# Selective scan in half groups: kept decays, one load a step, and a new order of GpSimd, TensorE and ScalarE work

## The chip, the cores and the metric

The kernel is one program on one core of a Trainium2 chip. The metric is the time on the device in microseconds (us), from the first to the last instruction of the run; less is better. The core has five engines that run side by side, each through its own instructions in order: TensorE (PE in the profile, its weight loads PEld), VectorE (DVE), ScalarE (ACT), GpSimd (POOL) and SyncE (SP), which here does nothing but issue DMA transfers. They meet only through semaphores: an instruction waits until another engine, or a DMA, has counted one up.

## The reference

Four images of 64 x 64 pixels and 96 channels go through four layers. The first is a Mamba-like layer, whose core is a selective scan over the L = 4096 pixels of an image, for 192 inner channels with 16 states each:

```python
def step(h, inp):
    u_t, dt_t, B_t, C_t = inp
    dA = jnp.exp(dt_t[..., None] * A)
    h = dA * h + (dt_t * u_t)[..., None] * B_t[:, None, :]
    y = jnp.sum(h * C_t[:, None, :], axis=-1)
    return (h, y)
```

It runs four times for an image: over the rows and over the columns, each forward and backward. The four results are added up, gated and projected. The layers after it are a 3 x 3 depthwise convolution with a pointwise one, linear attention with a feed-forward part in emulated fp8, and a frequency filter (Fourier transform, gate, inverse) with a second such feed-forward part.

## The kernel before, in words

**Half groups.** The scan takes 8 inner channels x 16 states = 128 partitions at a time. One `n` of the main loop (`for n in range(N + 1)`, N = 192) is one image, one order of the pixels (rows or columns) and one group of 8 channels, forward and backward. 24 values of `n` in a row share an image and an order; such a run of 24 is a half. The 4096 pixels are cut into four chunks `q` of 1024.

**Eight steps to an n.** Steps q0 to q3 are the forward scans of chunks 0 to 3 (VectorE, L1677, into S). Steps k0 to k3 are the backward scans of chunks 3, 2, 1, 0 (L1722, written over the decays), each followed by an addition of the backward states to S (L1729). The helpers around them are:

- `load_delta`, `load_du` (both issue at L1412): replicated loads. One chunk of 8 channels is spread over 128 partitions by two DMAs of 256 KB. `load_rep` (L1435) does it for B and C of a half, which stay for 24 values of n.
- `decay` (L1450): ScalarE, exp(dt * A) of a chunk from `dl` into a PSUM tile `pa` of two banks; there are two such tiles.
- `times_b` (L1440): GpSimd multiplies dt * u by B, in the tile `B`. `times_c` (L1444): GpSimd multiplies the summed states S by C.
- `reduce` (L1460): TensorE sums over the 16 states into the PSUM tile `py` (one bank, one buffer); `result` (L1468): ScalarE copies it out; `store_result` (L1477) sends it to memory.

PSUM is full: 4 banks for the two `pa` tiles, 1 for `py`, 3 for everything else. A forward scan of chunk 3 leaves its decays in PSUM for the backward scan; those of chunks 2, 1 and 0 are computed a second time. So there are seven `decay` calls to an n.

**The order is written out by hand.** Inside `tc.manual_schedule()` each engine runs the instructions as the loop emits them. The tiles of one tag reuse one buffer, so a load waits for the last reader of the chunk before it. `place_of` and the tag of `B` alternate with n, so that a chunk's place is free when the next half group's chunk needs it.

**Side work.** Everything else of the four images (projections and the 3 x 3 convolution ahead of the scans of an image, gating and all later layers after them) is cut into pieces, which two lanes hand out between the steps. `pieces(step)` gives each of five resources (TensorE, ScalarE, GpSimd, VectorE, the SP queue) a credit, in estimated us, from the table `gains`, one row for each of the eight steps; a piece is emitted when its resources have credit. ScalarE's copies of the pieces wait for TensorE's matmuls of the pieces, and stand in ScalarE's queue ahead of the next `decay`. Until about n = 54 the pieces are the projections and convolutions of images 1 to 3; later they are the layers after the scan of images 0 to 2. What is left of them after the last scan, and all later layers of image 3, run then: first `drain` with `last_post` (L619 to L625), then `tail`, which begins with the convolution L833.

Of the kernel before, what the change touches and what calls it, by code (L numbers as in the profile page):

```python
# [73 lines left out]
def layers(ctx: ExitStack, tc: tile.TileContext, a: dict, out):  # L74
# [1268 lines left out]
    def main_lane(take):  # L1343

        region = Region(tc)
        wk = region.sbuf("pre")
        images = [before_scans(b, wk, take, prev=b - 1 if b > 1 else None) for b in range(1, NB)]
        yield [chain(*parts) for parts in zip(*images)], [region, weights]
        for b in range(NB - 1):
            yield from rest(b, take, 1)  # L1350
# [17 lines left out]
    def last_place(name, k):  # L1368

        if (name, k) not in last_tiles:  # L1370
            tags = {
                "w_in": [f"B{4 * (N % 2) + q}" for q in range(4)],
                "sz_in": [f"dl{place_of(N - 1, q)}" for q in (3, 2, 1, 0)],
# [72 lines left out]
    def decay(n, q):  # L1446
        if n < N:
            pa = ps.tile([128, CH], F32, tag="pa", name="pa", bufs=2)
            g = phases[n][1]
            nc.scalar.activation(pa, dls[n, q], AF.Exp, scale=nega[:, g : g + 1])  # L1450
            return pa

    def reduce(n, half):
# [3 lines left out]
        py = pys[n, half] = ps.tile([128, BLK], F32, tag="py", name="py")  # L1457
        for j in range(4):
            q, k = 2 * half + j // 2, j % 2
            nc.tensor.matmul(  # L1460
                py[32 * j : 32 * j + 32, :], lhsT=red, rhs=Ss[n, q][:, k * BLK : (k + 1) * BLK],
                start=True, stop=True,
            )
# [19 lines left out]
    class Lane:  # L1483
# [133 lines left out]
    def first_loads():  # L1617
# [10 lines left out]
        for q in range(3):  # L1628
# [17 lines left out]
    with tc.manual_schedule():  # L1646
        ordered[0] = True
        pa = decay(0, 0)
        for n in range(N + 1):
# [3 lines left out]
            for q in range(NCH):  # L1653

                if q == 1:
                    load_du(n + 1, 3)
                if q > 1:
                    load_delta(n + 1, q - 2)
                if n % NG == 0 and 0 < n < N and q > 0:
                    load_rep(h, 1, 4 - q)  # L1660
                later = decay(n, q + 1) if q < 3 else decay(n, 2)
                if q == 0:
                    times_c(n - 1, 0)
                elif q == 1:
                    times_b(n, 3)
                else:
                    times_b(n + 1, q - 2)
                if q == 1:
                    reduce(n - 1, 0)
                if q == 2:  # L1670
                    store_result(n - 1, 1)
                if end:
# [5 lines left out]
                    s, pa, Bs[n, q], Ss[n, q - 1][:, CH - 1 : CH] if q else 0.0, ALU.mult, ALU.add  # L1678
                )
                if q < 3:  # L1680
                    pa = later
# [18 lines left out]
            for k, q in enumerate(reversed(range(NCH))):  # L1700
                if k == 0:
                    times_b(n + 1, 2)
                    result(n - 1, 0)
                    load_delta(n + 1, 2)
                else:
                    times_c(n, q + 1)
                if k == 1:
                    store_result(n - 1, 0)
                if k == 2:
                    load_delta(n + 1, 3)  # L1710
                if k > 0:
                    load_du(n + 2, k - 1)
                if n % NG == NG - 2:
                    load_rep(h + 1, 0, k)
                if k == 1:
                    pa, later = later, decay(n, 1)
                elif k == 2:
                    pa, later = later, decay(n, 0)
                elif k == 3:
                    pa, later = later, decay(n + 1, 0)  # L1720

                nc.vector.tensor_tensor_scan(  # L1722
                    pa[:, ::-1], pa[:, ::-1], Bs[n, q][:, ::-1],
                    edge if k else 0.0, ALU.mult, ALU.add,
                )
                if k < 3:
                    edge = big.tile([128, 1], F32, tag="edge", name="edge", bufs=2)
                    nc.vector.tensor_copy(edge, pa[:, 0:1])
                nc.vector.tensor_tensor(Ss[n, q], Ss[n, q], pa, ALU.add)  # L1729
# [6 lines left out]
            pa = later  # L1736
# [121 lines left out]
```

## Time and profile before

| | |
|---|---|
| time, median of 3 runs (lowest to highest) | 5908.66 us (5899.17 to 5910.47) |
| the profiled execution's own time | 5897.32 us |
| its span, first to last instruction | 5895.5 us |
| first and last scan begin at | 359.2 us, 5483.8 us |
| VectorE busy | 4947.4 us, 84% |
| GpSimd busy | 4104.8 us, 70% |
| TensorE busy | 4072.8 us, 69% |
| ScalarE busy | 3235.1 us, 55% |
| DMA queue of SP | 1169 MB, 71.7% of 16 engines |

A group of the profile is told by its line and engine, with output and inputs by name, the shape, the count, the busy time, the mean duration of one, and the idle time of the engine just before them with its main releaser. A row of waits says who waited for whom, for how long in total, how many times, and the longest. Some VectorE groups cost 1.2 to 2.4 us apiece, so a wait of a few tenths is small beside a step, and 192 of them are not small beside the total.

### The profile page before, as it was taken

The numbers are of one execution on the slowest core, as the hardware profiler recorded it, in microseconds if no ns is written. First come the engines' busy times: TensorE is split into PE (matmuls) and PEld (weight loads), VectorE is DVE, ScalarE is ACT, GpSimd is POOL, SyncE is SP. The second block draws the span as 40 slices with busy tenths as digits, with TensorE's granted clock in tenths as the row PEclk, the third lists the DMA queues.
The fourth block names the chain that finished last, engine by engine and source line by source line (L and its number), as shares of the span: only waits on it lengthen the run. The fifth ranks groups of instructions, "written<-read, shape, count | busy, mean of one in ns | idle before, by whom it ended". The sixth has DMA issues, their size and how long they took to land. (4 is left out here: it accounts for less than half of the span.)

```text
span 5895.5 us, 64395 instructions
## 1 busy us (share of the span) xinstructions
PE 4072.8 (69%) x19490; PEld 1646.2 (28%) x19490; DVE 4947.4 (84%) x3590; ACT 3235.1 (55%) x4358; POOL 4104.8 (70%) x1982
## 2 busy tenths in 40 slices
PE   8978888889873675553566764656467655566787
PEld 3322222223220121142321211433122114332245
DVE  2049898899899998999899999999998999989464
ACT  4557766776664356545555456454634554545333
POOL 1258888889898667767678778776866777766300
PEclk9978888889875765566657865676576655785788
DMA  3258878887698878788988868686986568896203
GB/s 99 77 158 236 226 208 223 244 243 206 187 248 238 229 199 222 202 227 246 254 228 229 211 169 222 203 239 187 239 224 182 158 190 234 248 242 184 57 30 112
DMA packets 469416, 1173.08 MB, mean 199 GB/s; under 512 B 90496, under 2 KB 155628, under 8 KB 468972
## 3 DMA queue, kind: packets, MB, share of 16 engines
q1 hardware_dynamic: 469068, 1168.97, 71.7%
q8 instruction: 154, 2.52, 0.2%
q14 instruction: 194, 1.59, 0.1%
HBM read 1011.86 MB, written 156.76 MB: 198 GB/s over the span
## 5 line engine op out<-in xcount | busy, mean ns | idle before, releaser
L1444 POOL TENSOR_TENSOR S<-S,rep 128x1024 f32<-128x1024 f32 x768 | 1807.1, 2353 | 965.1 <-DVE S L1729 885.1
L1450 ACT ACTIVATE pa<-dl,nega 128x1024 f32<-128x1024 f32 x1344 | 1498.5, 1116 | 1539.1 <-DVE S L1729 1175.0
L1440 POOL TENSOR_TENSOR B<-B,rep 128x1024 f32<-128x1024 f32 x768 | 1790.8, 2359 | 90.5 <-DMA B<-du_s 45.3
L1677 DVE TENSOR_TENSOR_SCAN S<-pa,S,B 128x1024 f32<-128x1024 f32 x576 | 1352.1, 2347 | 257.3 <-ACT pa L1450 86.1
L1722 DVE TENSOR_TENSOR_SCAN pa<-pa,edge,B 128x1024 f32<-128x1024 f32 x576 | 1354.0, 2351 | 66.7 <-ACT pa L1450 66.6
L1460 PE MATMUL py<-S,red 128*32 128x512 f32 x3072 | 630.9, 886 | 858.9 <-POOL S L1444 785.1
L361 PE MATMUL p_conv<-xp,conv_w 96*96 96x504 f32 (+3 forms) x2304 | 1056.4, 613 | 13.6 <-ACT u L374 11.5
L1729 DVE TENSOR_TENSOR S<-S,pa 128x1024 f32<-128x1024 f32 x768 | 932.2, 1214 | 6.6
L1677 DVE TENSOR_TENSOR_SCAN S<-pa,B 128x1024 f32<-128x1024 f32 x192 | 438.0, 2281 | 176.7 <-DMA rep<-bc_s 173.1
L361 PEld LDWEIGHTS p_conv<-xp,conv_w 96*96 96x96 f32 x2304 | 386.1, 171 | 669.0 <-issue 615.5
L1722 DVE TENSOR_TENSOR_SCAN pa<-pa,B 128x1024 f32<-128x1024 f32 x192 | 440.8, 2296 | 5.3
L1460 PEld LDWEIGHTS py<-S,red 128*32 128x32 f32 x3072 | 76.0, 128 | 1228.0 <-POOL S L1444 1009.6
L154 ACT COPY side<-side 96x256 f32<-96x256 f32 (+1 forms) x448 | 281.3, 628 | 52.9 <-DMA duT_s<-side 25.9
L1055 POOL CAST h<-y 128x1536 fp8e5<-128x1536 f16 x64 | 95.5, 1493 | 294.7 <-ACT y L766 284.2
L877 PE MATMUL p_mean<-t,centre 96*96 96x512 f32 x256 | 199.5, 895 | 117.7 <-ACT sq L869 48.8
L527 PE MATMUL p_y<-side,ident 96*96 96x512 f32 x336 | 215.2, 792 | 29.9 <-DMA side<-y_s 15.6
L1468 ACT COPY ys<-py 128x512 f32<-128x512 f32 x384 | 221.2, 576 | 19.6 <-PE py L1460 17.3
L929 PE MATMUL p_rstd<-rs_y,pick 32*96 32x512 f32 x256 | 168.4, 985 | 71.0 <-DVE ln L920 23.6
L833 PE MATMUL p_l<-x,taps 96*96 96x504 f32 (+3 forms) x432 | 202.8, 623 | 9.6 <-DMA x<-x 9.6
L1120 PE MATMUL p_h<-w1s,ln 97*64 97x64 f32 x2304 | 177.9, 346 | 36.7 <-DVE hb L1104 18.6
L1046 PE MATMUL p_f<-q,w_L 96*128 96x512 fp8e5 x192 | 98.2, 548 | 149.7 <-ACT y L757 75.6
L1120 PEld LDWEIGHTS p_h<-w1s,ln 97*64 97x64 f32 x2304 | 171.6, 251 | 78.2 <-issue 31.4
(210 smaller groups left out, 5059.4 us busy)
## 6 DMA issues: line engine op xcount, KB each, us to landing
dl<-delta_s SPq DMA_DIRECT2D x768, 256.0 KB
B<-du_s SPq DMA_DIRECT2D x768, 256.0 KB
B<-duT_s SPq DMA_DIRECT2D x768, 256.0 KB
dl<-deltaT_s SPq DMA_DIRECT2D x768, 256.0 KB
z_s<-z SPq DMA_DIRECT2D x48, 512.0 KB
zl<-z_s SPq DMA_DIRECT2D x64, 384.0 KB
side<-y_s SPq DMA_DIRECT2D x120, 192.0 KB
rep<-bc_s SPq DMA_DIRECT2D x64, 256.0 KB
```

The costliest lines, as they stand in the source:

```text
L154: nc.scalar.copy(o.rearrange("p (w h) -> p w h", h=HW), t[:n, :].rearrange("p (h w) -> p w h", w=HW)[:, q * w : (q + 1) * w, :],)
L361: nc.tensor.matmul(pr[:, ra:rb, ca_:cb_], lhsT=conv_w[:, kc, ky * 3 + kx, oc * C : (oc + 1) * C], rhs=xp[:, kc, at + ra : at + rb, ca_ + d ...
L527: nc.tensor.matmul(p, lhsT=ident[:C, :C], rhs=x, start=(j == 0), stop=(j == 2))
L1120: nc.tensor.matmul(p[at : at + N1, j, :], lhsT=ln3[:, 8 * k + j, :], rhs=w1s[:, hs], start=True, stop=True,)
L1440: nc.gpsimd.tensor_tensor(Bs[n, q], Bs[n, q], reps[n // NG, 0, q], ALU.mult)
L1444: nc.gpsimd.tensor_tensor(Ss[n, q], Ss[n, q], reps[n // NG, 1, q], ALU.mult)
L1450: nc.scalar.activation(pa, dls[n, q], AF.Exp, scale=nega[:, g : g + 1])
L1460: nc.tensor.matmul(py[32 * j : 32 * j + 32, :], lhsT=red, rhs=Ss[n, q][:, k * BLK : (k + 1) * BLK], start=True, stop=True,)
L1468: nc.scalar.copy(ys, pys.pop((n, half)))
L1677: nc.vector.tensor_tensor_scan(s, pa, Bs[n, q], Ss[n, q - 1][:, CH - 1 : CH] if q else 0.0, ALU.mult, ALU.add)
L1722: nc.vector.tensor_tensor_scan(pa[:, ::-1], pa[:, ::-1], Bs[n, q][:, ::-1], edge if k else 0.0, ALU.mult, ALU.add,)
L1729: nc.vector.tensor_tensor(Ss[n, q], Ss[n, q], pa, ALU.add)
```

## The change

- **Decays.** `decay` gets two tags of one buffer each, paX and paY, in place of one tag with two buffers, and a flag that tells which. The decays of chunk 2 are no longer computed a second time: those of chunks 2 and 3 both stay in PSUM from the forward scan to the backward one. Six calls remain to an n.
- **GpSimd.** Before, q0 to k3: C of the n before on chunk 0; B of chunk 3; B of the next n on chunk 0; on chunk 1; on chunk 2; C of chunk 3; of chunk 2; of chunk 1. After: q0 B of chunk 3; q1 C of the n before on chunk 0; q2 nothing; q3 B of the next n on chunk 0; k0 on chunk 1; k1 on chunk 2, and C of chunk 3; k2 C of chunk 2; k3 C of chunk 1.
- **TensorE.** The sum over chunks 0 and 1 of the n before, which stood in q1 as a whole, is split: chunk 1 in q1, chunk 0 in q3. ScalarE copies it out in k0, as before.
- **Loads.** Before: q1 du 3, q2 delta 0, q3 delta 1, k0 delta 2, k1 du 0, k2 delta 3 and du 1, k3 du 2 (the du of k1 to k3 are for the n after the next one, the others for the next). After: q0 du 2, q1 du 3, q2 delta 2, q3 delta 1, k0 delta 0, k1 du 0, k2 delta 3, k3 du 1.
- **Side work.** The table `gains` is new: TensorE's credit for an n stays 23.2 us, GpSimd's and VectorE's stay, ScalarE's rises from 14.3 to 15.5 us, SP's falls from 9.8 to 9.4 us. `sz_in` of the last image takes other tiles.

```diff
@@ -1370,7 +1371,7 @@
         if (name, k) not in last_tiles:
             tags = {
                 "w_in": [f"B{4 * (N % 2) + q}" for q in range(4)],
-                "sz_in": [f"dl{place_of(N - 1, q)}" for q in (3, 2, 1, 0)],
+                "sz_in": [f"dl{place_of(*x)}" for x in ((N - 1, 3), (N - 1, 2), (N - 1, 1), (N, 0))],
                 "xr": [f"rep0{q}" for q in range(4)],
                 "y_in": [f"B{4 - 4 * (N % 2) + q}" for q in range(4)],
             }
@@ -1443,19 +1444,23 @@
         if n >= 0:
             nc.gpsimd.tensor_tensor(Ss[n, q], Ss[n, q], reps[n // NG, 1, q], ALU.mult)
 
-    def decay(n, q):
+    def decay(n, q, first):
+
         if n < N:
-            pa = ps.tile([128, CH], F32, tag="pa", name="pa", bufs=2)
+            tag = "pa" + "XY"[(n + (not first)) % 2]
+            pa = ps.tile([128, CH], F32, tag=tag, name="pa")
             g = phases[n][1]
             nc.scalar.activation(pa, dls[n, q], AF.Exp, scale=nega[:, g : g + 1])
             return pa
 
-    def reduce(n, half):
+    def reduce(n, half, chunks=(0, 1)):
 
         if n < 0:
             return
-        py = pys[n, half] = ps.tile([128, BLK], F32, tag="py", name="py")
-        for j in range(4):
+        if (n, half) not in pys:
+            pys[n, half] = ps.tile([128, BLK], F32, tag="py", name="py")
+        py = pys[n, half]
+        for j in (2 * c + k for c in chunks for k in range(2)):
             q, k = 2 * half + j // 2, j % 2
             nc.tensor.matmul(
                 py[32 * j : 32 * j + 32, :], lhsT=red, rhs=Ss[n, q][:, k * BLK : (k + 1) * BLK],
@@ -1516,10 +1521,10 @@
     credit = [0.0] * 5
 
     gains = [
-        (2.6, 0.7, 0, 0.8, 1.8), (1.4, 1.2, 0, 0.8, 0.8),
-        (2.6, 1.2, 0, 0.8, 0.8), (2.6, 1.2, 0, 0.8, 0.8),
-        (3.8, 2.8, 1.2, 1, 1.6), (3.8, 2.4, 1.2, 1, 1.4),
-        (3.8, 2.4, 1.2, 1, 1.0), (2.6, 2.4, 1.2, 1, 1.6),
+        (2.6, 0.7, 0, 0.8, 1.4), (2.0, 1.2, 0, 0.8, 0.8),
+        (2.6, 1.2, 0, 0.8, 0.8), (2.0, 2.0, 0, 0.8, 0.8),
+        (3.8, 3.0, 1.2, 1, 1.4), (3.8, 2.6, 1.2, 1, 1.4),
+        (3.8, 2.4, 1.2, 1, 1.4), (2.6, 2.4, 1.2, 1, 1.4),
     ]
     cap = (4.4, 3.0, 3.2, 1.6, 4.0)
 
@@ -1625,7 +1630,7 @@
                 times_b(0, q)
         for q in range(NCH):
             load_rep(0, 1, q)
-        for q in range(3):
+        for q in range(2):
             load_du(1, q)
 
     wk = head.sbuf("pre0")
@@ -1645,40 +1650,40 @@
 
     with tc.manual_schedule():
         ordered[0] = True
-        pa = decay(0, 0)
+        pas = [decay(0, 0, True), None, None, None]
         for n in range(N + 1):
             h = n // NG
             end = n == N
 
             for q in range(NCH):
 
-                if q == 1:
-                    load_du(n + 1, 3)
-                if q > 1:
-                    load_delta(n + 1, q - 2)
+                if q < 2:
+                    load_du(n + 1, q + 2)
+                else:
+                    load_delta(n + 1, 4 - q)
                 if n % NG == 0 and 0 < n < N and q > 0:
                     load_rep(h, 1, 4 - q)
-                later = decay(n, q + 1) if q < 3 else decay(n, 2)
+                if q < 3:
+                    pas[q + 1] = decay(n, q + 1, q == 1)
                 if q == 0:
+                    times_b(n, 3)
+                elif q == 1:
                     times_c(n - 1, 0)
-                elif q == 1:
-                    times_b(n, 3)
+                    reduce(n - 1, 0, (1,))
+                elif q == 2:
+                    store_result(n - 1, 1)
                 else:
-                    times_b(n + 1, q - 2)
-                if q == 1:
-                    reduce(n - 1, 0)
-                if q == 2:
-                    store_result(n - 1, 1)
+                    times_b(n + 1, 0)
+                    reduce(n - 1, 0, (0,))
                 if end:
                     if q == 0:
                         result(n - 1, 1)
                     continue
                 s = Ss[n, q] = big.tile([128, CH], F32, tag=f"S{place_of(n, q)}", name="S")
                 nc.vector.tensor_tensor_scan(
-                    s, pa, Bs[n, q], Ss[n, q - 1][:, CH - 1 : CH] if q else 0.0, ALU.mult, ALU.add
+                    s, pas[q], Bs[n, q], Ss[n, q - 1][:, CH - 1 : CH] if q else 0.0,
+                    ALU.mult, ALU.add,
                 )
-                if q < 3:
-                    pa = later
                 pieces(q)
                 if q == 0:
                     result(n - 1, 1)
@@ -1698,42 +1703,45 @@
                 done["half", NB - 1] = True
 
             for k, q in enumerate(reversed(range(NCH))):
+                if k < 2:
+                    times_b(n + 1, k + 1)
+                if k > 0:
+                    times_c(n, q + 1)
                 if k == 0:
-                    times_b(n + 1, 2)
                     result(n - 1, 0)
-                    load_delta(n + 1, 2)
+                    load_delta(n + 1, 0)
+                elif k == 1:
+                    store_result(n - 1, 0)
+                    load_du(n + 2, 0)
+                elif k == 2:
+                    load_delta(n + 1, 3)
                 else:
-                    times_c(n, q + 1)
-                if k == 1:
-                    store_result(n - 1, 0)
-                if k == 2:
-                    load_delta(n + 1, 3)
-                if k > 0:
-                    load_du(n + 2, k - 1)
+                    load_du(n + 2, 1)
                 if n % NG == NG - 2:
                     load_rep(h + 1, 0, k)
                 if k == 1:
-                    pa, later = later, decay(n, 1)
+                    pas[1] = decay(n, 1, False)
                 elif k == 2:
-                    pa, later = later, decay(n, 0)
+                    pas[0] = decay(n, 0, True)
                 elif k == 3:
-                    pa, later = later, decay(n + 1, 0)
-
+                    first = decay(n + 1, 0, True)
+
+                to = pas[q]
                 nc.vector.tensor_tensor_scan(
-                    pa[:, ::-1], pa[:, ::-1], Bs[n, q][:, ::-1],
+                    to[:, ::-1], pas[q][:, ::-1], Bs[n, q][:, ::-1],
                     edge if k else 0.0, ALU.mult, ALU.add,
                 )
                 if k < 3:
                     edge = big.tile([128, 1], F32, tag="edge", name="edge", bufs=2)
-                    nc.vector.tensor_copy(edge, pa[:, 0:1])
-                nc.vector.tensor_tensor(Ss[n, q], Ss[n, q], pa, ALU.add)
+                    nc.vector.tensor_copy(edge, to[:, 0:1])
+                nc.vector.tensor_tensor(Ss[n, q], Ss[n, q], to, ALU.add)
                 if k == 3:
                     reduce(n, 1)
                 pieces(4 + k)
                 if n == N - 1:
                     for i in (2 * k, 2 * k + 1):
                         last_loads(last_place, i)
-            pa = later
+            pas[0] = first
             if n % NG == NG - 4 and h + 1 < len(halves):
                 b, o = halves[h + 1]
                 assert done.get(("turns", b)) if o else done.get(("back", b)) == NBLK, (n, done)
```

More of the change, by code (lines that the diff above doesn't have):

```diff
@@ L1348, in main_lane @@
         yield [chain(*parts) for parts in zip(*images)], [region, weights]
+        done["pre"] = True
         for b in range(NB - 1):
```

## The prediction

> **What bounds the kernel now.** First the page's busy times, then the loop of 192 half groups alone.
>
> ```profile
> PE 4072.8 (69%) x19490; PEld 1646.2 (28%) x19490; DVE 4947.4 (84%) x3590; ACT 3235.1 (55%) x4358; POOL 4104.8 (70%) x1982
> 360.00:5487.00 5127.00, 3415.42 (x15469) 1330.48 (x15469) 4723.67 (x3211) 2913.81 (x3879) 3976.40 (x1882) 0.71 0.79 218
> ```
>
> The second line is the table of stretches: from the first scan to the last addition VectorE is busy 4723.7 of 5127 us. Its rows L1677, L1722, L1728 and L1729 add up to 4608 us, 24.0 us a half group, while a half group takes 26.7 us. The change removes no VectorE instruction, so it can win only from the 403 us in which VectorE stands idle there, and from what lies before (359 us) and after (409 us).
>
> Next, whom VectorE waits for, and whom ScalarE, TensorE and SP wait for (us in total, times, longest):
>
> ```profile
> DVE S L1677 <- ACT pa L1450: 88.5, 59, 8.7
> DVE pa L1722 <- ACT pa L1450: 66.6, 38, 7.8
> DVE S L1677 <- DVE S L1677: 30.6, 122, 0.5
> DVE S L1677 <- PE py L1460: 21.0, 13, 4.6
> ACT sz L343 <- PE p_z L337: 64.3, 19, 10.0
> ACT os L757 <- PE p_o L1183: 73.5, 37, 6.6
> PE py L1460 <- POOL S L1444: 785.1, 171, 15.6
> SPq L1435 <- POOL B L1440: 40.2, 6, 11.7
> ```
>
> Late decays are the largest item, 155 us. But ScalarE is only 55% busy. In the timeline most of the long stalls follow a ScalarE copy that stood waiting for TensorE, with the decay queued behind it. One of them, step q3 of n = 183:
>
> ```profile
> 5237.87 1.06 PE L1460 MATMUL py<-S,red 128*32 128x512 f32 x8
> ...
> 5241.76 0.49 ACT L757 ACTIVATE os<-p_o 128x384 f32<-128x384 f32 x1 [6.59 <-PE p_o L1183]
> 5242.15 2.15 ACT L1450 ACTIVATE pa<-dl,nega 128x1024 f32<-128x1024 f32 x2
> 5243.35 2.35 DVE L1677 TENSOR_TENSOR_SCAN S<-pa,S,B 128x1024 f32<-128x1024 f32 x1 [4.73 <-ACT pa L1450]
> ```
>
> TensorE comes to the sums of q1, waits there for GpSimd's C of chunk 0, and only then does the p_o that ScalarE wants; two decays run late and the scan stands for 4.73 us. Taking VectorE's timeline scan by scan, waits above 0.4 us, less 0.2 us that a scan with satisfied waits loses too, come to 192 us: 104 in n = 1 to 55 and 89 after. By step: q1 37, q2 18, q3 76, k2 17, k3 42, q0 3. The waits under 0.4 us, some 100 us, stay: each forward scan waits for its predecessor.
>
> Below, a place in an n is counted in steps by VectorE's scan starts: 0 is the start of q0, 4 that of k0, 8 that of the next n; 1.03 is just past the start of q1. A step is 2.4 us (q) or 3.6 us (k).
>
> **What the Trainium skill says.** TensorE: Matmul & The Clock Gate, Architectural detail: ScalarE and VectorE are strict FIFOs. The trace agrees (decays behind os). PSUM — Partial Sum Buffer, Specifications: eight banks of 2 KiB a partition; that is why only two chunks' decays fit, and the two new tags take the same four banks. ScalarE: Activation LUTs, Rules for kernel authors: 0.3 us and 0.83 ns an element, by estimate 1.15 us for 1024; the trace has 1.116. DMA: Bandwidth & Descriptors, Anatomy of one DMA: about 2 us fixed plus bytes / 436 GB/s, 2.6 us for 256 KB by estimate; here the issue and landing stamps give 3.0 us at best and about 5 in the median, since many share the queue, so I use 5.
>
> **Part by part.**
>
> *Decays.* 192 x 1.116 = 214 us leave ScalarE. It had slack, so this alone buys nothing but room. The removed decay stood at q3, was done a step before k1 needed it, and showed no stall (k1: one wait, 0.5 us). About half of it is filled at once: ScalarE's credit rises by 1.2 us an n.
>
> *The split sum.* At q1 TensorE now needs only chunk 1, whose C was done in k3 of the n before. The C of chunk 0 starts at 0.1 steps of n in the median and takes 2.35 us (0.65 step); TensorE stands until then in the later part (median start 1.03 steps). After the change that sum stands at q3, and the C of chunk 0, behind B of chunk 3, ends near step 1.7: no wait. If GpSimd had a 1.5 us cast and more in between, there is still a step of cover. The buffer of chunk 0's S is wanted again only at the next q0, that of chunk 1 at q3, for which its sum now comes earlier. Exposed to it are the ScalarE and TensorE waits at q2 and q3 after n = 55: 30.8 + 9.7 + 2.7 = 43 us. I take two thirds: -29.
>
> *B of chunk 3 first.* It was due at step 3 and waited behind C; the POOL B waits of the scans are 11 us. At each change of half SP's load of B's chunk 3 waits for exactly this multiplication (40.2 us over 6 of 7 turns, everything behind it late), and the two half groups on either side hold 49 of the 192 us. One step earlier: -10.
>
> *Early part.* Its 104 us are mostly k3 and q1, behind copies that wait for TensorE running convolutions at 3.8 us of credit in steps of 3.6 us (p_z, up to 10.0 us). Credits there stay; only the freed ScalarE time helps: -15. The k2 and k3 stalls later (20 us): -5.
>
> *Loads.* delta 0 moves from q2 to k0, needed at k3. The load that stood at k0 was issued at step 3.9 and landed at 5.2 in the median, 6.9 at 90%, 8.2 at 99%; needed at 7.0, harmful from 7.7. On SP it stands behind the stores of q2 (which wait for ScalarE's copy) and delta 1 (which waits for decay 3), ahead of the store of k1. If it is late, ScalarE stands at k3 with that piece work behind it, and q0 of the next n is late. Two to four in a hundred late by about a us: +4. Bounds: 0, since it waits for one decay less, and 20. The du loads gain a step or more; delta 2 gains two; delta 3 keeps its place, with one load fewer behind it.
>
> *Copy at k0.* It now needs a sum that was made two steps later. Later than n = 55 TensorE is at most one step late (90%: 1.83 for slot 1), so done by 3.9, and the copy came at 3.7 in the median: +5, bounds 0 and 80 (a rival below).
>
> *What remains after the last scan.* The order in which the two kernels emit their work shows the side lanes some 3 n later in the new one: after the last scan 8 blocks of image 2's last feed-forward remain in place of 2. That adds to the stretch before L833: TensorE 15 x 0.53 + 18 x 0.59 + 4 x 0.99 = 23 us, GpSimd 6 x 1.56 + 5 x 1.28 = 16 us, VectorE and ScalarE about 16 each. The stretch is 35 us with TensorE busy 21 and GpSimd 15.5:
>
> ```profile
> 5487.00:5522.00 35.00, 21.07 (x34) 5.52 (x34) 21.14 (x27) 8.07 (x15) 15.52 (x11) 0.56 0.30 85
> ```
>
> At least 21 + 23 - 35 = 9 us; at most six blocks at the 4.2 us a block that image 3's last feed-forward takes (33.4 us for 8), 25. I take +17. The loop loses some 5 products by p_rstd and their likes on VectorE: -4.
>
> Sum: -29 - 10 - 15 - 5 - 4 + 4 + 5 + 17 = -37 us. On the profiled execution, 5897.3 (span 5895.5), that is 5860; the median of the runs is 11.3 us above it, so 5872; I say 5870.
>
> **Rivals.**
> 1. *Waits on ScalarE go as a class.* If the freed time and the unblocked TensorE take two thirds of all ACT stalls (the 127 us of the 192), -85, with -10 for the turns and +26 against: 5840. For: each stall has ScalarE last. Against: most are behind TensorE or a DMA.
> 2. *No change.* The stalls come from where pieces happen to meet; new credits draw them anew. Gains of about 25 us against 26 of costs: 5908.
> 3. *Slower: the copy at k0 becomes the wait.* In n under 54 TensorE reaches the sums of q1 at 1.94 steps in the median and 2.65 at 90%, a step or more late. At q3 that is 3.9 to 4.7, while ScalarE is there at 3.7: it stands 0.7 to 3.5 us, with the long gate piece of k0 and the decay for k2 behind it, and SP's store behind it too. At 1.5 us in 54 half groups, +80 in place of +5: 5945. It decides from 42 us on, 0.8 us in each of these n. For: PE is 87% busy up to 1600 us. Against: k2 is two steps away, and such a copy waits now only 17.3 us in 8 times.
>
> **Chances and range.** My sum 0.41 (its own range 5850 to 5896), the first rival 0.27, no change 0.12, slower 0.20. 0.2%, 12 us, is about what a measurement can tell: faster 0.68, same 0.12, slower 0.20. From 5805 (all of rival 1 and no cost after the scans) to 5930 (half of rival 3) leaves out 2 in 10.
>
> **What would show it.** Right: 1152 decays; TensorE's wait on POOL at the sums well below 785 us; VectorE's waits on L1450's successor below 120 us, most of the loss at q3; SP's wait for the chunk-3 B shorter; the stretch from last scan to L833 longer by 9 to 25 us. Wrong: ScalarE's wait for py above 60 us, waits for delta 0 at q0, or k2 and k3 stalls that grow.

## The result, and the profile after

The changed kernel is slower: 5962.48 us (median of 4 runs, 5959.17 to 5968.03) against 5905.83 us for the kernel before beside it (4 runs, 5899.17 to 5910.47), a ratio of 1.0100 with a 95% interval of 1.0084 to 1.0116. The forecast was 5870 us, its range ended at 5930. The profiled execution took 5959.17 us (span 5957.4). Set beside the one of before by the marks of the program, its 61.9 us more lie here:

| | before | after | |
|---|---|---|---|
| to the first scan | 359.2 | 357.7 | -1.5 |
| first scan to the end of the last addition | 5128.2 | 5152.1 | +23.9 |
| last addition to the first convolution L833 of the tail | 34.5 | 67.5 | +33.0 |
| from there to the end | 373.6 | 380.1 | +6.5 |

So the kernel lost in the loop, where 54 us were to be won, and in the stretch behind the loop it lost 33 us in place of 17. A single execution can lie 13 us from the median of its kernel (5938.11 against 5924.98 us for one of the experiments), so what a part of the change is worth is read from medians and ratios below, and from profiles only where it sits. The busy times of the page:

```profile
PE 4259.6 (72%) x19490; PEld 1666.0 (28%) x19490; DVE 4960.4 (83%) x3613; ACT 3023.2 (51%) x4144; POOL 4099.0 (69%) x1981
```

ScalarE lost 212 us, as the forecast said. TensorE gained 187 us of busy time with the same 19490 instructions; the forecast says nothing of that. The table of stretches (length, then busy time of TensorE, weight load, VectorE, ScalarE, GpSimd, the granted clock of TensorE as a share of full speed, DMA share, GB/s), first the stretch before L833, then the tail:

```profile
5509.80:5577.30 67.50, 42.34 (x74) 11.21 (x74) 38.24 (x55) 23.51 (x39) 34.60 (x23) 0.58 0.18 50
5577.30:5957.00 379.70, 324.32 (x3242) 191.93 (x3242) 166.77 (x250) 114.28 (x196) 26.98 (x23) 0.86 0.17 56
```

In the stretch every engine has about the extra work that was forecast (TensorE 21 us, GpSimd 20, VectorE 17, ScalarE 16), but no engine is busy more than 63% of it. And the waits of the whole kernel that answer to those shown of before:

```profile
DVE S L1683 <- ACT pa L1453: 90.5, 53, 4.9
DVE pa L1730 <- ACT pa L1453: 92.1, 47, 6.8
DVE S L1683 <- DVE S L1683: 44.2, 174, 0.7
DVE S L1683 <- POOL B L1441: 25.9, 35, 8.3
DVE S L1683 <- PE py L1465: 18.9, 18, 3.3
ACT sz L343 <- PE p_z L337: 32.8, 17, 5.5
ACT os L757 <- PE p_o L1183: 84.4, 41, 6.9
ACT ys L1473 <- PE py L1465: 260.8, 99, 9.7
PE py L1465 <- POOL S L1445: 564.6, 114, 15.1
PE py L1465 <- ACT ys L1473: 151.4, 43, 7.2
SPq L1436 <- POOL B L1441: 31.1, 9, 9.8
```

TensorE waits 220 us less for GpSimd, as forecast, and SP less for the B of chunk 3. But VectorE waits for late decays longer than before (183 us against 155), and two rows are new in size: ScalarE's copy `ys` waits 260.8 us for the sum `py`, and TensorE 151.4 us for that copy. The same two rows before:

```profile
ACT ys L1468 <- PE py L1460: 17.3, 8, 5.0
PE py L1460 <- ACT ys L1468: 13.9, 4, 6.2
```

VectorE's stalls before its scans, counted as in the prediction (waits above 0.4 us, less 0.2 us), in us by step:

| kernel | q0 | q1 | q2 | q3 | k2 | k3 | sum |
|---|---|---|---|---|---|---|---|
| before | 3 | 37 | 18 | 85 | 17 | 42 | 201 |
| after | 22 | 25 | 26 | 82 | 74 | 9 | 236 |

(k0 and k1 are below 0.5 us in both.) This count takes in n = 0, where the scan of chunk 3 waits 8.7 us before the change and 8.3 after; without it the sums are 192 us, as in the prediction, and 228. What left k3 came out at k2, q0 is new, and q3, from which most of the gain was to come, stands where it was.

One of the stalls at k2, in n = 15; a line is start, duration, engine and instruction, with the wait before it in brackets:

```profile
766.59 5.23 PE L361 MATMUL p_conv<-xp,conv_w 96*96 96x504 f32 x11
...
771.75 1.05 PE L1465 MATMUL py<-S,red 128*32 128x512 f32 x4
...
772.85 0.58 ACT L1473 COPY ys<-py 128x512 f32<-128x512 f32 x1 [8.43 <-PE py L1465]
...
776.77 1.11 ACT L1453 ACTIVATE pa<-dl,nega 128x1024 f32<-128x1024 f32 x1
...
777.91 2.36 DVE L1730 TENSOR_TENSOR_SCAN pa<-pa,edge,B 128x1024 f32<-128x1024 f32 x1 [5.60 <-ACT pa L1453]
```

TensorE has convolutions to do and comes to the second half of the split sum at 771.75; ScalarE has stood 8.43 us at the copy, with five pieces and the decay queued behind it, and VectorE's scan stands 5.60 us. This is the third rival's mechanism. In n below 54 that half of the sum starts at 4.12 steps in the median. But the wait does not end there: from n = 55 on this half ends later than step 3.9 in 44 of 137 half groups, and ScalarE's copy of it waits 116 us in 54 of them, after 136 us in 39 before. VectorE's stalls at k2 grew from 8 to 51 us up to n = 54, and from 9 to 22 us after.

### The profile page after: what moved, and what is told of

The parts are those of the page before. It is cut to its first block, busy times and chain, and to the rows that moved or that the text cites. A ratio compares the mean times of both kernels' runs of the same rounds, so it can differ in the third digit from the quotient of the medians.

```text
span 5957.4 us, 63603 instructions
## 1 busy us (share of the span) xinstructions
PE 4259.6 (72%) x19490; PEld 1666.0 (28%) x19490; DVE 4960.4 (83%) x3613; ACT 3023.2 (51%) x4144; POOL 4099.0 (69%) x1981
## 5 line engine op out<-in xcount | busy, mean ns | idle before, releaser
L1453 ACT ACTIVATE pa<-dl,nega 128x1024 f32<-128x1024 f32 x1152 | 1285.3, 1117 | 1485.4 <-DVE S L1737 1148.2
L1465 PE MATMUL py<-S,red 128*32 128x512 f32 x3072 | 871.1, 855 | 784.8 <-POOL S L1445 564.6
L1465 PEld LDWEIGHTS py<-S,red 128*32 128x32 f32 x3072 | 104.9, 126 | 1279.5 <-POOL S L1445 731.4
L1473 ACT COPY ys<-py 128x512 f32<-128x512 f32 x384 | 222.5, 579 | 302.8 <-PE py L1465 260.8
L833 PE MATMUL p_l<-x,taps 96*96 96x504 f32 (+3 forms) x432 | 207.6, 635 | 12.8 <-DMA x<-x 12.8
```

The lines of the kernel that those rows point to most:

```text
L1465: nc.tensor.matmul(py[32 * j : 32 * j + 32, :], lhsT=red, rhs=Ss[n, q][:, k * BLK : (k + 1) * BLK], start=True, stop=True,)
L1473: nc.scalar.copy(ys, pys.pop((n, half)))
```

## The experiments

Each kernel ran beside the kernel before on the same chip. Differences between two kernels are differences of their ratios, with the half widths of both intervals added in squares; 0.1% is 5.9 us.

**Which part costs.** `sp_credit_back`: only SP's column of the table as before.

```diff
-        (2.6, 0.7, 0, 0.8, 1.4), (2.0, 1.2, 0, 0.8, 0.8),
+        (2.6, 0.7, 0, 0.8, 1.8), (2.0, 1.2, 0, 0.8, 0.8),
         (2.6, 1.2, 0, 0.8, 0.8), (2.0, 2.0, 0, 0.8, 0.8),
-        (3.8, 3.0, 1.2, 1, 1.4), (3.8, 2.6, 1.2, 1, 1.4),
-        (3.8, 2.4, 1.2, 1, 1.4), (2.6, 2.4, 1.2, 1, 1.4),
+        (3.8, 3.0, 1.2, 1, 1.6), (3.8, 2.6, 1.2, 1, 1.4),
+        (3.8, 2.4, 1.2, 1, 1.0), (2.6, 2.4, 1.2, 1, 1.6),
```

> The changed kernel with SP's column of the credits as it was (9.8 us an n in place of 9.4), nothing else. As emitted, 2 blocks of image 2's last feed-forward are then left after the last scan, as before the change, in place of 8. Theory (two separate costs: blocks left over, and ScalarE's copy of the split sum at k0): the stretch from last scan to L833 goes from 67 us back to 33 to 37, the whole to about 5925; the loop stays at 5150 (within 15 us), k2's stalls near 80 us, ScalarE's wait for py near 260 us. Rival (the leftover is hidden and the tail is long for another reason): the stretch stays above 60 us and the time at 5960.

Measured: 5924.98 us, ratio 1.0030 (1.0017 to 1.0043), so 0.70 +- 0.21%, 41 us, of the loss is gone. The stretch before L833 in the table of stretches of this kernel:

```profile
5530.00:5563.20 33.20, 21.37 (x32) 5.44 (x31) 19.05 (x26) 7.42 (x13) 13.64 (x10) 0.52 0.24 72
```

It is again as short as before the change (34.5 us): 0.4 us less credit an n on SP's queue leaves six blocks more over. ScalarE's wait for py stays (270.5 us, 89 times). The loop of this profile, 5173.5 us, is longer than the 5150 expected; its execution lies 13 us above the median.

`copy_in_k1`: the changed kernel, ScalarE's copy of the split sum in k1 behind the decay, its store in k2.

```diff
                 if k == 0:
-                    result(n - 1, 0)
                     load_delta(n + 1, 0)
...
                 if k == 1:
                     pas[1] = decay(n, 1, False)
+                    result(n - 1, 0)
```

> The changed kernel with ScalarE's copy of the sums of chunks 0 and 1 moved from k0 to k1, behind the decay for k2, and its store from k1 to k2. Theory: the copy at k0 holds up the decay for k2; then k2's stalls fall from 81 us to 30 or less, ScalarE's wait for py from 261 us to under 100, the loop from 5152 to about 5105, the whole to about 5915; the blocks left over and the stretch of 67 us stay. Rival (ScalarE's larger credits fill its queue ahead of the decays): k2's stalls stay above 60 us, the loop above 5140.

Measured: 5948.76 us, 1.0064 (1.0048 to 1.0080): 0.36 +- 0.23%, 21 us. The wait is gone and k2 falls from 74 to 47 us, less than the theory's 30, and the time stays well above its 5915 us; up to n = 54 k2 falls from 51 to 23 us, after that it does not fall (22 and 24):

```profile
ACT ys L1473 <- PE py L1465: 12.0, 7, 2.9
```

`old_credits`: the changed kernel with the whole table of before.

> The changed kernel with the whole table of credits as before the change. Theory: the stretch after the last scan is 33 to 37 us again, but the loop keeps its loss (k2's stalls above 60 us, ScalarE's wait for py above 200 us): about 5920. Rival (the larger credits of ScalarE make the loop's loss): the loop falls below 5128 and k2's stalls below 35 us; the whole 5895 or less.

Measured: 5932.28 us, 1.0033 (1.0023 to 1.0043), the same as with SP's column alone (0.03 +- 0.16% apart). That the larger credits of ScalarE and the moved ones of TensorE win or lose anything is not seen.

`credit_and_copy_back`: both edits at once.

> The changed kernel with two of its parts taken back: SP's column of credits as before, and ScalarE's copy of py in k1 instead of k0. If the two costs are separate and add, 5962 - 37 - 14 = 5911 us, the stretch from the last addition to the first tail convolution near 33 us, ScalarE's wait of ys for py below 30 us and VectorE's stalls at k2 near 50 us. If the copy's cost was only borrowed from the left-over blocks (fewer blocks left over leave more of them to run inside the steps, where they get in the way of the copy's gain), 5925 us as with the credit alone. Below 5900 would mean that the rest of the change is a gain that these two parts hid.

Measured: 5900.4 us, 0.9983 (0.9972 to 0.9994), 1.17 +- 0.19% below the changed kernel; the two alone give 1.06%. They add, within what can be told, and together they are the whole loss: the rest of the change is a gain of 0.17 +- 0.11%.

**The parts alone, on the kernel before.** `keep_decays_alone`: two tags, six decays, everything else as before.

```diff
-                later = decay(n, q + 1) if q < 3 else decay(n, 2)
+                if q < 3:
+                    pas[q + 1] = decay(n, q + 1, q == 1)
...
```

> The kernel before with one part of the change alone: the decays of chunk 2 stay in PSUM, six decays to an n; loads, sums, GpSimd and credits as before. Theory (freed ScalarE time is only slack, since the decays that come late stand behind copies that wait for TensorE): 5890 to 5905, stalls on decays 155 us down to 125 to 150. Rival A (ScalarE's time matters): below 5875. Rival B (the kept tiles themselves cost the loop, a wait for a buffer): above 5920.

Measured: 5903.8 us, 0.9990 (0.9982 to 0.9997). Taking 214 us from ScalarE is worth 6 us (2 to 11). `loads_alone`: that kernel with the new order of the loads.

> The kernel before with the kept decays and the new order of the replicated loads alone; credits, GpSimd's order and the sums as before. Theory (the loads are harmless, delta 0 lands well before its decay): 5904 us, as with the kept decays alone, stalls at q0 below 6 us. Rival (the 20 us of new stalls at q0 come from the loads): stalls at q0 near 20 us and 5915 to 5925 us.

Measured: 5915.1 us, 1.0004 (0.9995 to 1.0012), 0.14 +- 0.11% more than without. Stalls at q0 are 22 us against 2: here the rival was right on the place. ScalarE's waits for delta in this kernel (72.5 us in the kernel before, 98 with the kept decays alone):

```profile
ACT pa L1451 <- DMA dl<-deltaT_s: 93.2, 18, 8.7
ACT pa L1451 <- DMA dl<-delta_s: 80.7, 16, 10.8
```

`gpsimd_and_split`: the changed kernel with loads and credits of before, so kept decays, GpSimd's new order and the split sum.

> The changed kernel with the loads and the credits as before: kept decays, GpSimd's new order and the split sum with its copy at k0. Theory (the new order on GpSimd with the split sum makes what the loop lost): 5925 us, ScalarE's wait of ys for py above 200 us, stalls at k2 above 55 us. Rival (the loss comes from the loads): 5904 us or less, stalls at k2 below 30 us.

Measured: 5925.68 us, 1.0025 (1.0015 to 1.0034), stalls at q0 1.9 us, at k2 59 us, wait for py 250.5 us. That is 0.35 +- 0.12% or 21 us more than with the kept decays alone: most of what the loop lost comes from here, and the copy at k0, worth about as much above, is part of it.

`whole_sum_q2`: the changed kernel with the old credits and the sum of both chunks whole, in q2.

```diff
-                    reduce(n - 1, 0, (1,))
                 elif q == 2:
+                    reduce(n - 1, 0)
                     store_result(n - 1, 1)
...
-                    reduce(n - 1, 0, (0,))
```

> The changed kernel with the credits as before and the sum of chunks 0 and 1 issued whole in q2, its copy still at k0. If it is the second half of the split sum that comes too late for the copy, the whole sum in q2 is no later than that (it waits for the same chunk 1 of S C): wait of ys for py stays above 200 us and 5930 us. If splitting itself delays TensorE (convolutions that get between the halves), the wait falls below 100 us, stalls at k2 below 35 us, 5915 us.

Measured: 5942.52 us, 1.0053 (1.0037 to 1.0070). Both expectations missed: the wait for py falls to 68.6 us and k2 to 3.5 us, but q3 stalls 204 us. The timeline says why (n = 8):

```profile
575.56 8.26 PE L361 MATMUL p_conv<-xp,conv_w 96*96 96x512 f32 x12 [0.61 <-ACT u L374]
...
583.75 1.06 PE L1465 MATMUL py<-S,red 128*32 128x512 f32 x8
...
584.88 0.59 ACT L1473 COPY ys<-py 128x512 f32<-128x512 f32 x1 [6.46 <-PE py L1465]
585.03 2.35 DVE L1682 TENSOR_TENSOR_SCAN S<-pa,S,B 128x1024 f32<-128x1024 f32 x1 [7.64 <-PE py L1465]
```

The scan of chunk 3 writes the buffer in which chunk 1 of the n before stood (`place_of`), and must wait until TensorE has summed that. A later sum only moves the wait from ScalarE's queue to VectorE's own. The half of chunk 1 has to stand in q1.

**What took the place of the wait for GpSimd.** The forecast held that at q1 TensorE would find all it needs. In the changed kernel it finds chunk 1, but not `py`, which has one bank and one buffer. Step q1 to q3 of n = 93, changed kernel:

```profile
2841.25 0.62 ACT L154 COPY side<-side 96x256 f32<-96x256 f32 x1 [3.52 <-DMA deltaT_s<-side]
...
2842.27 0.57 ACT L1473 COPY ys<-py 128x512 f32<-128x512 f32 x1
...
2842.94 1.92 PE L1465 MATMUL py<-S,red 128*32 128x512 f32 x4 [7.90 <-issue]
...
2848.56 0.49 ACT L757 ACTIVATE os<-p_o 128x384 f32<-128x384 f32 x1 [3.86 <-PE p_o L1183]
...
2850.14 2.35 DVE L1683 TENSOR_TENSOR_SCAN S<-pa,S,B 128x1024 f32<-128x1024 f32 x1 [3.85 <-DMA dl<-delta_s]
```

ScalarE's copy of the sum over chunks 2 and 3 stands in q0 behind the pieces, one of which waits for a DMA. It ends at 2842.84, and 0.1 us later TensorE, idle for 7.9 us, begins the sum of q1. Then the stall of the prediction's example follows as before: p_o late, ScalarE late, scan late. The wait is put down to "issue", and the scan's to a DMA; the order in time tells more than the names. Take TensorE's idle time ahead of the sum of q1 (the whole sum before, chunk 1 after), from n = 55 on, in waits that end during VectorE's steps q0 and q1, by which of the two ended last: before, GpSimd's C 224 us and the copy 69; after, the copy all of the 200 us, and it ended 0.1 us ahead of the sum in all 77 waits. "Perfetto Trace Analysis" of the Trainium skill, Optimizing Tensor Performance, Matmuls, says that independent groups of matmuls should rotate through different banks of PSUM so that the evacuation of one overlaps the next. Here two such groups share one bank, and TensorE's 200 us of idle time agree with the page; how much of it costs time is another question. A second bank was not tried.

`early_copy`: on `credit_and_copy_back`, the copy in q0 ahead of the pieces.

```diff
+                if q == 0:
+                    result(n - 1, 1)
                 pieces(q)
-                if q == 0:
-                    result(n - 1, 1)
```

> As the run with credit and copy taken back, and in q0 ScalarE copies out the sum over chunks 2 and 3 ahead of the pieces of the step instead of behind them. Theory: after the change TensorE's sum of chunk 1 in q1 no longer waits for GpSimd but for this copy, since py has one buffer; with n from 55 on these waits at q0 and q1 are 249 us (in the kernel before 224 us for GpSimd and 69 for the copy). The earlier copy takes most of that away: below 80 us, stalls at q3 down from 72 to about 50 us, and 5885 us. Rival (the sum in k3 is not ready that early, so ScalarE now stands for TensorE, with the pieces of q0 and the decay for q2 behind it): wait of ys for py above 60 us, stalls at q1 and q2 above 70 us together, 5905 us or more.

Measured: 5882.33 us, 0.9953 (0.9940 to 0.9966), 0.30 +- 0.17% or 18 us better than without. Stalls at q3 are 63 us against 72. Of the waits for the copy those at q1 go (77 to 4 us), those at q0 don't (172 to 200): there TensorE runs a step ahead of VectorE. So the expectation had the size of the wait wrong (below 80 us) and the time nearly right.

`keep_and_early_copy`: the same edit on the kernel before with the kept decays.

> The kernel before with the kept decays alone, and the earlier copy of the sum over chunks 2 and 3 in q0 on top; sums, GpSimd, loads and credits as before. Theory (in the old order the sum in q1 waits for GpSimd's C of chunk 0, 224 us against 69 for the copy, so an earlier copy can free only the smaller part): 5900 us, gain over the kept decays alone below 6 us, TensorE's waits for C at q0 and q1 still above 220 us. Rival (the earlier copy is a gain of its own): 18 us as in the new order, 5886 us, stalls at q3 down from 93 to 80 us.

Measured: 5897.5 us, 0.9975 (0.9964 to 0.9987), 0.15 +- 0.14% better than the kept decays alone. That lies between theory and rival: by these medians about half of the 18 us would come in the old order too, though the intervals don't exclude that all of it would. TensorE waits 247 us there for C at q0 and q1 all the same.

**GpSimd's order and the loads.** `early_copy_c_first`: `early_copy` with C of chunk 0 in q0 and B of chunk 3 in q1.

```diff
                 if q == 0:
-                    times_b(n, 3)
+                    times_c(n - 1, 0)
                 elif q == 1:
-                    times_c(n - 1, 0)
+                    times_b(n, 3)
```

> The run with the earlier copy, with GpSimd's first two multiplications swapped back: C of chunk 0 of the n before in q0, B of chunk 3 in q1. Theory (B first is worth what the forecast said, late Bs at q3 and at the turns of halves): 5892 us, 10 us slower, SP's wait for that B above 30 us. Rival (nothing waits for either within a step, the order is worth nothing): 5882 us, within 5 us.

Measured: 5890.58 us, 0.9970 (0.9959 to 0.9981), 0.17 +- 0.17% or 10 us slower, at the edge of what can be told; q3 goes from 63 to 75 us and SP's wait for the B of chunk 3 from 22.6 to this:

```profile
SPq L1436 <- POOL B L1441: 41.4, 16, 10.2
```

Four kernels try the loads. `loads_back_too` is `credit_and_copy_back` with all loads in the old order, `delta_order_back` has delta 0 in q2 and delta 2 in k0 alone; `early_copy_loads_back` and `early_copy_delta_back` are the same on `early_copy`. The edit of the delta loads:

```diff
-                    load_delta(n + 1, 4 - q)
+                    load_delta(n + 1, q - 2)
...
                 if k == 0:
-                    load_delta(n + 1, 0)
+                    load_delta(n + 1, 2)
```

> As the run with credit and copy taken back, and the replicated loads in their old order too (delta 0 in q2, delta 2 in k0, du as before). Theory (delta 0 in k0 arrives too late for some of the decays that q0 waits for): stalls at q0 fall from 30 to below 6 us, ScalarE's waits for delta from 178 us to about 100, and the time by some 8 us, as the loads alone cost: 5892 us. Rival (the stalls at q0 only come out at other steps): 5900 us again, with the sum of the stalls where it was, 212 us.

> As the run with credit and copy taken back, with delta 0 in q2 and delta 2 in k0 as in the kernel before, and the du loads in the new order. Theory (it is delta 0 alone): stalls at q0 below 8 us and the time of the run with all loads back, 5892 us. Rival (the new order of the du loads, or that there is one load fewer at a time in front of others, does it): stalls at q0 stay near 25 us and 5900 us.

> Both: the earlier copy of the sum over chunks 2 and 3, and the old order of the loads, on the run with credit and copy taken back. If the two gains are there and add: 5877 us. If only the loads' is: 5892 us; if neither: 5900 us.

> The run with the earlier copy, with delta 0 in q2 and delta 2 in k0 as in the kernel before. If delta 0 in k0 costs what the two runs without the earlier copy show (0.17%, 10 us): 5872 us, stalls at q0 near 13 us. If that difference was a chance of how pieces fall, as the run with all loads back suggests: 5882 to 5895 us.

| | as changed | all loads back | delta back |
|---|---|---|---|
| on `credit_and_copy_back` | 0.9983 | 0.9987 (0.9979 to 0.9994), 5900.65 us | 0.9966 (0.9952 to 0.9979), 5888.7 us |
| on `early_copy` | 0.9953 | 0.9967 (0.9954 to 0.9979), 5895.22 us | 0.9936 (0.9924 to 0.9948), 5871.03 us |

Delta 0 in k0 (and delta 2 in q2) costs 0.17% both times (together 0.17 +- 0.12%, 10 us); stalls at q0 go from 30 and 25 us to 13 and 11. That all loads back win nothing says that the new order of du is worth as much as delta 0 costs or more (0.21 +- 0.16% and 0.31 +- 0.17% between the last two columns); why was not tried. For `loads_back_too` the rival held: q0 fell to 8 us, q2 rose from 31 to 47, and the time stayed. `early_copy_loads_back` missed the 5877 us of two gains that add.

`early_copy_delta_back`, at 5871.03 us (6 runs, 5865.99 to 5878.97), is faster than both kernels: 0.64% below the kernel before, interval 0.52 to 0.76%. Against `keep_and_early_copy`, which has the kept decays and the early copy in the old order, it is 0.39 +- 0.17% or 23 us faster: so much are GpSimd's new order, the split sum with its copy in k1, the du loads and the other credits worth together, once what spoiled them is out. No run has the split sum without the rest, so its own share is not known.

**The price of a split sum.** TensorE's 187 us more come from the sums, which took 240 us more; the rest of its work took 53 less. The groups of TensorE in the page, before and after, and then of `full_width_sums` (count, busy time, mean ns of one, idle time before):

```profile
L1460 PE MATMUL py<-S,red 128*32 128x512 f32 x3072 | 630.9, 886 | 858.9 <-POOL S L1444 785.1
```

```profile
L1465 PE MATMUL py<-S,red 128*32 128x512 f32 x3072 | 871.1, 855 | 784.8 <-POOL S L1445 564.6
```

```profile
L1466 PE MATMUL py<-S,red 128*32 128x256 f32 x6144 | 656.6, 527 | 816.0 <-POOL S L1445 598.8
```

The eight instructions of a whole sum take 1.06 us (n = 183, in the prediction's example); the four of half a sum take 1.05 us too (771.75 above, where the trace grants the clock 1.00), and 1.92 us at a granted clock of 0.50 (2842.94 above; a whole sum then takes 1.93). Each fp32 matmul is two instructions of the trace. Each writes 32 partitions of PSUM; the four of a whole sum start within 0.02 us and run side by side, each 0.617 us, twice over. A chunk alone has two, for half of TensorE's columns, and takes as long. "TensorE: Matmul & The Clock Gate" of the Trainium skill, Why this matters for your kernels, says it: outputs at partitions 32j fall into different column groups, which run at the same time; the trace agrees. By the busy times a split costs (871 - 631) / 192 = 1.25 us of TensorE in every n.

`full_width_sums`: the changed kernel, a chunk cut into four blocks of 256 for four column groups; the store writes the pieces of 256 where they belong, in runs of 1 KB instead of 2 KB.

```diff
-        for j in (2 * c + k for c in chunks for k in range(2)):
-            q, k = 2 * half + j // 2, j % 2
-            nc.tensor.matmul(
-                py[32 * j : 32 * j + 32, :], lhsT=red, rhs=Ss[n, q][:, k * BLK : (k + 1) * BLK],
-                start=True, stop=True,
-            )
+        w = BLK // 2
+        for c in chunks:
+            for j in range(4):
+                nc.tensor.matmul(
+                    py[32 * j : 32 * j + 32, c * w : (c + 1) * w], lhsT=red,
+                    rhs=Ss[n, 2 * half + c][:, j * w : (j + 1) * w], start=True, stop=True,
+                )
...
```

> The changed kernel; only the sum of a chunk is cut into four blocks of 256 pixels, for the four column groups of TensorE, in place of two blocks of 512 for two of them (the store to memory follows). Theory: the split sum cost TensorE twice the time, since a chunk alone fills two of the four groups: four records take 1.05 us at full clock, as eight do, so an n costs 1.25 us more (busy time of the sums 871 us in place of 631 before). With four groups that is gone: the sums' busy time below 680 us, ScalarE's wait of ys for py from 261 to below 130 us, stalls at k2 from 74 to about 45 us, and 5962 - 21 = 5941 us or a little less (the left-over blocks stay). Rival (the copy's wait comes from its place alone, TensorE being late in any case): wait above 220 us, 5960 us.

Measured: 5937.48 us, 1.0054 (1.0042 to 1.0066): 0.46 +- 0.20% or 27 us better than the changed kernel. The sums take 656.6 us, stalls at k2 fall from 74 to 53 us; the wait for py falls only to 211.5 us, not below 130. So the width is part of why the copy in k0 waits, and its place is the other part. `full_width_best`: the same on `early_copy_delta_back`.

> The run with the earlier copy and the order of delta taken back, with the sums cut into blocks of 256 pixels for all four column groups. Theory: TensorE wins 240 us over the loop, 1.25 us an n; up to n = 54, where it is the engine that the others wait for, that takes 15 us of the 116 us of stalls, later some 5 us: 5851 us. Rival (TensorE's time at the sums lies beside VectorE's steps): 5871 us.

Measured: 5880.51 us, 0.9964 (0.9947 to 0.9982), 0.28 +- 0.21% or 16 us worse than without. The sums take 661 us in place of 874, and no time comes of it. With the copy in k1 ScalarE hardly waits for the sums (25.7 us, 28.4 without the edit), which fits the rival: TensorE's 1.25 us lie beside VectorE's steps, and the width costs only where somebody stands behind it. The rival doesn't explain why the kernel became slower; loads land as soon as without the edit (4.6 us in the median of both), and whether the shorter runs of the store are the cause was not tried.

## Why the prediction was wrong

The forecast had +22 us for the copy at k0 and the left-over blocks, and the runs with these two taken back show +69; it had -59 us for all the rest, and the runs show -10. So costs that were put too low and gains that did not come have about equal parts in the miss (+57 us measured, -37 forecast). By its own steps:

- **Decays** (0): right. 1152 decays, 1285 us, and alone worth 6 us. The scans of k1 never waited. (The credit's 1.2 us an n is all of the 1.1 us that was freed, and not half of it, as the prediction has it; `old_credits` shows no effect of that credit.)
- **Split sum** (-29): failed, and this is the first of the steps that decided. Its sentence "at q1 TensorE now needs only chunk 1" leaves out that the sum needs `py` empty. The wait for C went as forecast (224 us to none), and the wait for the copy rose from 69 to 200 us; q3 kept its stalls. With the copy ahead of the pieces 18 us came, of which about half seem to belong to the copy in any order. It also took the split as free for TensorE, where it costs 1.25 us an n. (A C of 2.35 us is not 0.65 of a step of q but nearly a whole one: it ends at 0.97 before the change, at 1.4 in the median and 2.2 at 90% after it, still in time for q3.)
- **B of chunk 3 first** (-10): supported, 10 us, though only just beyond what can be told; SP's wait shorter, as said.
- **Early part** (-15): failed. Freed time on ScalarE moved nothing there: 102 us of stalls in n = 1 to 55 with the kept decays alone, 104 before. In the changed kernel they are 121, and 101 with the copy in k1.
- **Later k2 and k3** (-5): failed. After n = 55 k3 fell from 11 to 6 us, and k2 rose from 9 to 22.
- **Delta 0** (+4, bounds 0 and 20): inside the bounds, 10 us. Loads landed as forecast (6.9 steps at 90%, 7.8 at 99%), yet a few late ones stop ScalarE for 8 to 10 us each (n = 152, 154, 184 to 186), and VectorE's scan of q0 then waits 1.9 to 4.8 us, where the forecast had about one.
- **Copy at k0** (+5, bounds 0 and 80): mis-sized, 21 +- 13 us by taking it away in the changed kernel, 28 +- 10 us between `sp_credit_back` and `credit_and_copy_back`. Its step "so done by 3.9" did not hold even after n = 55, where it was made: in 44 of 137 half groups the sum ended later (4.5 at 90%). Up to n = 54 the half sum came at 4.1 steps in the median, the number that the third rival had worked out (3.9 to 4.7). That rival had the mechanism and put it at 80 us; the copy waits 252 us in 93 half groups for this sum, but most of a wait has slack behind it, and only the stalls at k2 up to n = 54 fall when the copy is moved. It did not reach the 42 us at which it was to decide the sign.
- **Left-over blocks** (+17, bounds 9 and 25): mis-sized, and of the two costs the larger. The stretch grew by 33 us, and taking SP's credit back wins 41 +- 12. The eight blocks run from 5529 to 5577 us, 6 us each, not 4.2. The last of them, on TensorE, ScalarE, VectorE, GpSimd and TensorE again:

```profile
5569.89 0.40 PE L1046 MATMUL p_f<-q,w_L 96*128 96x512 fp8e5 x1
5570.33 0.60 ACT L757 ACTIVATE y<-p_f 128x512 f16<-128x512 f32 x1 [0.67 <-PE p_f L1046]
...
5572.24 0.33 DVE L768 TENSOR_SCALAR y<-y,b_L 128x512 f16<-128x512 f16 x1
5573.53 1.46 POOL L1055 CAST h<-y 128x1536 fp8e5<-128x1536 f16 x1
...
5575.04 1.44 PE L1066 MATMUL p_f<-h,w_L 128*96 128x512 fp8e5 x3 [4.75 <-POOL h L1055]
5576.59 0.69 DVE L761 CAST z<-p_f 96x512 f16<-96x512 f32 x1 [1.45 <-PE p_f L1066]
...
5577.33 3.49 PE L833 MATMUL p_l<-side,taps 96*96 96x512 f32 x4 [0.85 <-DVE z L761]
```

The end of one block alone is a chain of 7.4 us through four engines. The forecast bounded it by busy time (TensorE 23 us) and by the rate of a stage in which many blocks overlap; here the blocks share the stretch with other work on each of those engines and end one by one.
- **p_rstd** (-4): not measured by itself.

Of the signs that were to show it right, 1152 decays and the shorter waits of TensorE for GpSimd and of SP came; fewer waits for decays and a stretch of at most 25 us more did not. All that were to show it wrong came as well: the wait for py (261 us), waits for delta 0 at q0, and stalls at k2 and k3 that grow (59 to 82 us together). The third rival had the sign, and part of that was luck: its mechanism is worth 21 to 28 us, too little for a loss by itself, and it said nothing of longer left-over work. The ends of the forecast's range also don't come out of its terms: all 127 us of the first rival with no cost after the scans give about 5780 us, not 5805, and half of the third rival's 80 us about 5907, not 5930.

## What to carry to other kernels

An engine waits for several things at once, and the profile names one: before a wait is counted as won, list every other condition of that instruction (its output buffer above all) and when each is met. Cutting a sum in two is not free for TensorE where its matmuls run side by side in column groups; count the groups that each part fills. And blocks of side work that fall out of an overlapped loop can cost more than their busy time, here 6 us a block with no engine busy more than 63%: look at the length of their chain. Here 0.4 us of credit an n cost 41 us.

## What the runs showed of the hardware that was not expected

Four fp32 matmuls of 128 x 32 by 512 to four quarters of PSUM's partitions take 1.06 us together, and two take 1.05 us, at a granted clock of 1.00. Loads of 256 KB whose landing times looked harmless (median 5.3 steps, 99% at 7.8, needed at 7.0) stopped ScalarE for up to 10.2 us in single half groups (n = 152). Taking 214 us of work from an engine that is 55% busy was worth 6 us (2 to 11), although that engine was the last one named in 155 us of VectorE's waits.
